# Row maxima of an adjacency matrix: two full passes, or one pass over segments and a gathered window

## The chip, the core and the metric

The kernel runs on one core of a Trainium2 chip. The metric is device time in microseconds (us) of one execution, lower is better. A profile is one execution taken by the hardware profiler; its engines are PE (TensorE's matrix products; PEld its weight loads), DVE (VectorE), ACT (ScalarE), POOL (GpSimd, which here issues the gathers) and SP (which issues most other transfers).

## The reference

Four graph layers on 2708 nodes of 512 features, with one adjacency matrix `adj` (2708x2708, f32, sparse, with a positive diagonal). Cut to what is computed:

```python
# layer 0
h = maximum(layernorm(x), 0)
head = (adj > 0) / max(sqrt(count of adj > 0 in the row), 1e-12)
x = x + ((adj + head) @ h) / rowsum(adj + head)
# layer 1: attention, 8 heads of 64
h = maximum(layernorm(x), 0)
a = maximum(adj, eye)
atts = softmax(q @ k.T / 8 - 1e16 * (1 - a))
x = x + sum over heads (atts @ v) @ Wo
# layer 2
h = maximum(layernorm(x), 0)
h = relu(adj @ (h @ W1) + b1); h = relu(adj @ (h @ W3) + b3)
x = x + tanh(h @ Wf + bf)
# layer 3
h = maximum(layernorm(x), 0)
A = (adj != 0)
x = x + (A @ (h @ W + b)) / colsum(A)
```

The mask of layer 1 multiplies `1 - a` by 1e16, so each row's softmax puts all its weight on the row's largest entry of `max(adj, eye)`. The kernel therefore needs, for each row, the place of that maximum, and the two largest values to see that the maximum stands clear (where it does not, a general version of the whole computation runs, behind a condition at the end; it does not run on these inputs). Layer 1 then is a gather: row i of the result is row `idx[i]` of a table `y = h @ Wv @ Wo`.

## The kernel before, in words

The 2708 rows are 22 row tiles of 128 (the last has 20). Layer 0 goes through the row tiles `m` in a loop (L854). Columns of `adj` that hold many non-zeros are multiplied as whole tiles (`WHOLE[m]` of them); of the rest only the source rows with a non-zero are taken: the kernel counts and ranks them, searches their numbers (`search`, L448, FIND_INDEX8 over a row of ranks), and gathers per row tile `CHUNKS[m]` (5 to 10) pieces of `adj` transposed (`gather_adj`, L635, tile `ac`, 128 runs of 512 bytes) and as many of `h` (`gather_rows`, L654, tile `h`, 16 buffers). Both are indirect DMAs issued by POOL, which works through its list in order. TensorE multiplies the pieces at L866 into `acc`.

Everything that needs a whole row tile of `adj` as rows runs ahead of this loop. `stats_to(k)` (L762) works through the tiles in `order_n` up to tile k: it loads the tile as a slab `ar` (128x2708 f32, three buffers, `load_slab`, L563), takes signs, counts and sums on ScalarE (`row_norm`, `row_sum`), counts columns on TensorE for each group of three (`count`, L325, copied by ScalarE at L341 to L345) and ranks them (`rank_blocks`, L399 to L405, with a small product on TensorE at L403), and then calls `attended`:

```python
nc.vector.tensor_max(ar[:n, cols], ar[:n, cols], ident[:n, :n])
nc.vector.max(tops[:n, m, :], ar[:n])
nc.vector.max_index(at_top[:n, m, :], tops[:n, m, :], ar[:n])
```

L622 is the maximum with the identity on the diagonal block. L623 is one VectorE instruction (MAX8) that gives the eight largest values of 2708; L624 is two, a load of the eight values (MATCH_VALUE_LOAD) and a search for their places (FIND_INDEX8), again over 2708. Six tiles (`LATE`: 3, 4, 5, 0, 1, 2) do not call `attended` in `stats_to`; their slabs are loaded a second time in the last eight turns of the loop (L890 to L895, with `count_signs` on ScalarE).

Behind the loop the places become `idx` (L914), which layer 1's gather of `y` uses (`fetch`, L1172, on POOL); `flags` (L278) compares the two largest values. `after` computes `y` two tiles behind (L176, copied at L810), with a transpose at L210. `norm` (L194 to L204) normalizes the finished rows, first scaled and added at L879. `incidence` builds TensorE's operands on VectorE (L698, L706).

A framework orders the instructions: it records them as the Python program issues them, with their dependencies, and sorts each engine's list by priority and by its own estimate of when each can start. The order on each engine is fixed when the kernel is built. Waits between engines, and between an instruction and the result of another of its own engine, are semaphores that the framework sets. `with tc.issue_after(ins):` adds an edge: what the block issues on `ins`'s engine stands behind `ins` in that engine's list. Tiles of a pool with `bufs=k` take turns in k buffers; a tile that takes a buffer waits until all that used the one before are done.

Of the kernel before, what the change touches and what calls it, by code (L numbers as in the profile page):

```python
# [9 lines left out]
FP = mybir.dt.float32  # L10
# [3 lines left out]
U32 = mybir.dt.uint32  # L14
U8 = mybir.dt.uint8
I32 = mybir.dt.int32
AF = mybir.ActivationFunctionType
ALU = mybir.AluOpType
AX = mybir.AxisListType
# [3 lines left out]
P = 128  # L23
LN_EPS = 1e-5
NORM_EPS = 1e-12
MASK_SCALE = 1e16
# [18 lines left out]
def kernel(  # L45
# [27 lines left out]
    nc = tc.nc  # L73

    N, D = x.shape
    H, _, DK = wk_d.shape
    NT = (N + P - 1) // P
    NFULL = N // P
# [4 lines left out]
    UNIT = 4  # L83
# [81 lines left out]
    nc.gpsimd.memset(ones_b, 1.0)  # L165


    adj_units = bass.AP(adj_t.tensor, 0, [[UNIT, N * N // UNIT], [1, UNIT]])

    def span(t):  # L170
# [73 lines left out]
    with tc.tile_pool(name="l0_slab", bufs=2) as slabs, tc.tile_pool(  # L244
# [15 lines left out]

        idx_a = hp.tile([P, NT, NCH], U32, name="idx_a")

        tops = hp.tile([P, NT, 8], FP, name="tops")
        at_top = hp.tile([P, NT, 8], U32, name="at_top")
        cnts, sums_sgn, ends, caps = (
            hp.tile([P, NT], FP, name=name) for name in ("cnts", "sums_sgn", "ends", "caps")
        )
# [5 lines left out]
        if TAIL:  # L273
            nc.gpsimd.memset(tops[:, NFULL, :], 0.0)
            nc.gpsimd.memset(tops[:, NFULL, 0:1], 2.0)
            nc.gpsimd.memset(at_top[:, NFULL, :], 0)

        def flags():  # L278

            score = wp.tile([P, NT, 2], FP, name="score", bufs=1)  # L280
            nc.vector.tensor_scalar(
                score, tops[:, :, 0:2], 1.0, MASK_SCALE, op0=ALU.subtract, op1=ALU.mult
            )
            nc.vector.tensor_tensor(bad[:, :NT], score[:, :, 1], score[:, :, 0], ALU.is_ge)
            nc.vector.tensor_tensor(
                bad[:, BAD_NEG : BAD_NEG + NT], sums_sgn, cnts, ALU.not_equal
            )
            nc.vector.tensor_tensor(bad[:, BAD_MANY : BAD_MANY + NT], ends, caps, ALU.is_gt)
# [17 lines left out]
        nc.gpsimd.iota(place_i, pattern=[[P, NCH]], base=1, channel_multiplier=1)  # L306
        places = hp.tile([P, NCH], FP, name="places")
        nc.vector.tensor_copy(places, place_i)

        pending, pending_c = [], []  # L310

# [253 lines left out]
        def count_signs(m, last):  # L565

            sgn = slabs.tile([P, N], BF, name="sgn", bufs=GROUP)
            behind(sgn[:1, :1], last)
            nc.scalar.activation(sgn, slab[m], AF.Sign, accum_out=sums_sgn[:, m : m + 1])
            nc.scalar.activation(sgn, sgn, AF.Relu, accum_out=cnts[:, m : m + 1])  # L570
# [46 lines left out]
        def attended(m):  # L617

            n = rows(m)
            cols = slice(m * P, m * P + n)  # L620
            ar = slab.pop(m)
            nc.vector.tensor_max(ar[:n, cols], ar[:n, cols], ident[:n, :n])  # L622
            nc.vector.max(tops[:n, m, :], ar[:n])  # L623
            nc.vector.max_index(at_top[:n, m, :], tops[:n, m, :], ar[:n])  # L624

        gathers, gather_slot = {}, [0]

# [134 lines left out]
        def stats_to(m):  # L762


            while normed[0] <= order_n.index(m):
                t = order_n[normed[0]]
                do_next()
                load_slab(t)
                if normed[0] + 1 < NT:
                    load_slab(order_n[normed[0] + 1])  # L770
                row_norm(t)
                row_sum(t)
                if t == 0 or t % GROUP == GROUP - 1 or t >= NT - 2:
                    last_block = count(masks)
                    if t not in ZERO:
                        if dense_of(t):
                            rank_blocks(list(masks), last_block)
                        else:
                            flush_counts()
                            todo.append(partial(rank_rows, list(masks)))  # L780
                        todo.extend(partial(search, k) for k in masks)
                        do_next(0)
                    masks.clear()
                if t in LATE:
                    slab.pop(t)
                else:
                    attended(t)
                normed[0] += 1
# [65 lines left out]
        for m in range(NT):  # L854
            n = rows(m)
            if m + 1 < NT:
                load_x(m + 1)
            if m + 2 < NT and m + 2 >= LEAD and dense_of(m + 2):
                blocks[m + 2] = load_block(m + 2, tiles_d[: min(dense_of(m + 2), PIECE0)])
            flush()  # L860
            if LEAD <= m + 1 < NT:
                incs[m + 1] = incidence(m + 1)
            acc = ps_acc.tile([P, D], FP, name="acc")
            pairs = incs.pop(m)
            for i, (a, g) in enumerate(pairs):
                product = nc.tensor.matmul(  # L866
                    acc[:n], a, g, start=(i == 0), stop=(i == len(pairs) - 1)
                )
                first_of_sum = first_of_sum if i else product.ins
            if m + 1 < LEAD:  # L870
                stats_to(m + 1)
                incs[m + 1] = incidence(m + 1)
            if m > 1:
                with tc.issue_after(first_of_sum):
                    after(m - 2, None)
            if m:
                after(m - 1, hns.pop(m - 1))
            xt = xs.pop(m)
            nc.vector.scalar_tensor_tensor(  # L879
                xt[:n], acc[:n], row.pop(m)[1][:n], xt[:n], op0=ALU.mult, op1=ALU.add  # L880
            )
            hns[m] = wp.tile([P, D], FP, name="hn")
            norm(wp, xt, n, hns[m])
            store(m, xt)
            if normed[0] == NT:
                do_next(2 if NT - 8 < m < NT - 5 else 1)
            stats_to(min(2 * m + 6, m + 8, NT - 1))
            gathers_to(m + 2)

            step = m - (NT - 8)  # L890
            if 0 <= step < len(LATE):
                load_slab(LATE[step])
            if 0 < step <= len(LATE):
                count_signs(LATE[step - 1], xt[:1, :1])
                attended(LATE[step - 1])  # L895
            if m + 8 == NT + 1:
                todo.append(partial(rank_rows, list(range(1, LEAD))))
                todo.extend(partial(search, k) for k in range(1, LEAD))
            if m == NT // 2:
                load_scores(xt[:1, :1])  # L900
            if m == NT // 2 + 2:
                score_bound(xt[:1, :1])
            if m == NT - LEAD - 1:
                for t in range(1, LEAD):
                    gather_adj(t)
            if m == NT // 2 + 3:
                wr = load_w(wset, w1_d, "wr", lambda w: behind(w[:1, 0, :1], xt[:1, :1]))
            if m == NT // 2 + 5:
                w1 = split_w(
                    wset, wr, "wa", lambda w: behind(w[:1, :1], xt[:1, :1])  # L910
                )
                wr = load_w(wset, w3_d, "wr")
        flush()
        nc.vector.tensor_copy(idx, at_top[:, :, 0])  # L914
        degrees()
        after(NT - 2, None)
        after(NT - 1, hns.pop(NT - 1))
# [1035 lines left out]
```

## Time and profile before

| what | value |
|---|---|
| runs | 1424.02, 1426.85, 1431.88 us; median 1426.85 |
| the profiled execution: its own time, and its span from first to last instruction | 1431.05 us, 1429.2 us |
| mean granted TensorE clock (1 is full speed) | 0.925 |
| PE busy, share of the span | 1218.8 us, 85% |
| DVE | 924.7 us, 65% |
| ACT | 693.2 us, 49% |
| POOL | 673.6 us, 47% |
| layer 0 (0 to 515 us): DVE busy from 100 to 515 | 325.2 us |
| POOL busy from 100 to 515 | 241.7 us |
| L622, L623, L624: first and last start | 99.0 and 498.1 us |

The span is that of the instructions; the own time has a little more around it. Busy time counts no register, branch, semaphore and DMA-issuing instructions of the sequencers. Matmuls are pipelined and their ends are modelled, so a busy PE is not a PE at its peak. In lines of groups the columns are: line, engine, operation, output<-inputs, shape, count | busy us, mean ns of one | idle time of the engine before them and what ended most of it. In a timeline they are start, duration, engine, line, operation, output<-inputs, shape, count and, in brackets, the idle time in front and what ended it.

### The profile page before, as it was taken

What the parts mean: (1) busy time and instruction counts of PE and PEld (TensorE: products, weight loads), DVE (VectorE), ACT (ScalarE), POOL (GpSimd) and SP (SyncE); (2) the same over time, 40 slices, a digit from 0 to 9 for tenths busy, and PEclk for the clock granted to TensorE, in tenths of its full rate; (3) what the DMA queues carried; (4) which work ended last, traced back from release to release, by engine and by line L of the source; (5) the groups of instructions that cost most, each with busy time, mean ns of one, the idle gap of its engine ahead of it and who ended that gap; (6) DMA issues with size and microseconds to landing.
All of it is one profiled execution on the core that took longest, in us unless ns stands there. A gap on an engine that the chain in (4) does not pass through costs nothing. (4 is left out here: it accounts for less than half of the span.)

```text
span 1429.2 us, 15148 instructions
## 1 busy us (share of the span) xinstructions
PE 1218.8 (85%) x4223; PEld 726.3 (51%) x4223; DVE 924.7 (65%) x1859; ACT 693.2 (49%) x1098; POOL 673.6 (47%) x703
## 2 busy tenths in 40 slices
PE   4985977769896848999989999899999999958797
PEld 2332433324343326765655655466666666646575
DVE  4664977768899857952343446356667685746576
ACT  5873563648635636642232224245555554634353
POOL 2245457555667441116645543245445344167663
PEclk9977998789988969999999999999999999979898
DMA  9976898778979477638888887856566666488785
GB/s 342 350 251 225 283 302 277 246 249 293 322 253 335 168 254 266 220 128 272 259 261 255 274 248 239 273 177 219 194 212 193 198 190 207 137 313 249 248 250 163
DMA packets 179342, 349.92 MB, mean 245 GB/s; under 512 B 22795, under 2 KB 85525, under 8 KB 175517
## 3 DMA queue, kind: packets, MB, share of 16 engines
q1 hardware_dynamic: 131648, 201.72, 41.5%
q0 software_dynamic: 46032, 145.05, 32.6%
q10 hardware_dynamic: 1568, 2.10, 0.4%
q8 instruction: 35, 0.57, 0.2%
q14 instruction: 59, 0.48, 0.1%
HBM read 285.97 MB, written 62.82 MB: 244 GB/s over the span
## 5 line engine op out<-in xcount | busy, mean ns | idle before, releaser
L1047 POOL DMA_INDIRECT gg<-g2d,idx_g x130 | 141.2, 1086 | 197.1 <-PE aggs L1110 149.3
L1110 PE MATMUL aggs<-gg,ac 128*128 128x512 f32 (+1 forms) x520 | 231.3, 593 | 3.2 <-DMA gg<-g1d,idx_g 2.1
L1047 POOL DMA_INDIRECT gg<-g1d,idx_g x130 | 130.7, 1005 | 159.1 <-PE aggs L1110 86.5
L635 POOL DMA_INDIRECT ac<-in_adj_t_dram,idx_a x130 | 132.7, 1021 | 91.9 <-issue 37.3
L866 PE MATMUL acc<-h,inc 128*128 128x512 f32 (+1 forms) x276 | 143.0, 664 | 37.4 <-DVE inc L706 29.2
L1110 PEld LDWEIGHTS aggs<-gg,ac 128*128 128x128 f32 (+1 forms) x520 | 97.0, 188 | 113.6 <-issue 102.2
L654 POOL DMA_INDIRECT h<-h0d,idx_g x111 | 114.8, 1034 | 83.7 <-PE acc L866 40.8
L866 PE MATMUL acc<-h,incl 128*128 128x512 f32 (+1 forms) x222 | 106.0, 620 | 0.8 <-issue 0.8
L866 PEld LDWEIGHTS acc<-h,inc 128*128 128x128 f32 (+1 forms) x276 | 54.9, 212 | 101.0 <-issue 60.2
L1075 DVE SCALAR_TENSOR_TENSOR ac<-ac,diag_c,bias 128x512 f32<-128x512 f32 x30 | 22.6, 754 | 100.8 <-DMA ac<-g1d 59.1
L1047 POOL DMA_INDIRECT gg<-hidr,idx_g x62 | 70.7, 1140 | 34.6 <-issue 20.8
L176 PE MATMUL yacc<-wvo,hT 128*128 128x512 f32 (+1 forms) x176 | 83.9, 615 | 1.7 <-ACT hT L211 1.0
L1106 PE MATMUL agg<-ghi,a_hi 128*128 128x512 f32 x180 | 77.3, 429 | 0.0
L1106 PE MATMUL agg<-glo,a_lo 128*128 128x512 f32 x180 | 73.4, 408 | 4.2 <-ACT glo L225 4.2
L1106 PE MATMUL aggs<-gs,a_s 128*128 128x512 f32 x180 | 73.1, 406 | 1.3 <-DVE gs L222 1.3
L990 DVE SCALAR_TENSOR_TENSOR v_lo<-pt,v_hi 128x512 fp32r<-128x512 f32 (+1 forms) x88 | 57.0, 658 | 16.2 <-ACT v_hi L989 13.9
L866 PEld LDWEIGHTS acc<-h,incl 128*128 128x128 f32 (+1 forms) x222 | 41.8, 195 | 50.0 <-issue 47.1
L623 DVE MAX8 tops<-ar 128x8 f32<-128x2708 f32 (+1 forms) x22 | 65.4, 2971 | 0.0
L624 DVE FIND_INDEX8 at_top<-tops,ar 128x8 uint32<-128x2708 f32 (+1 forms) x22 | 65.3, 2969 | 0.0
L989 ACT ACTIVATE v_hi<-pt 128x512 fp32r<-128x512 f32 (+1 forms) x88 | 48.2, 575 | 29.0 <-PE pt L983 22.1
L1139 DVE SCALAR_TENSOR_TENSOR u<-aggs,u 128x512 f32<-128x512 f32 x42 | 28.9, 687 | 50.9 <-PE aggs L1110 37.7
L1010 PE MATMUL main<-wb,v_hi 128*128 128x512 f32 (+1 forms) x176 | 56.7, 444 | 5.2 <-ACT v_hi L989 3.4
(355 smaller groups left out, 2777.9 us busy)
## 6 DMA issues: line engine op xcount, KB each, us to landing
ar<-in_adj_dram SPq DMA_DIRECT2D x27, 1354.0 KB
raw<-in_adj_t_dram SPq DMA_DIRECT2D x92, 192.0 KB
slot<-x SPq DMA_DIRECT2D x41, 256.0 KB
at<-in_adj_t_dram SPq DMA_DIRECT2D x26, 256.0 KB
h<-in_x_dram SPq DMA_DIRECT2D x21, 256.0 KB
h0d<-h POOLq DMA_DIRECT2D x21, 256.0 KB
xt<-in_x_dram SPq DMA_DIRECT2D x21, 256.0 KB
x<-xt SPq DMA_DIRECT2D x21, 256.0 KB
```

What stands on the lines that cost most here:

```text
L176: nc.tensor.matmul(acc[:n], hT[:, c, :n], w[:, c, :], start=(c == 0), stop=(c == NCD - 1))
L623: nc.vector.max(tops[:n, m, :], ar[:n])
L624: nc.vector.max_index(at_top[:n, m, :], tops[:n, m, :], ar[:n])
L635: nc.gpsimd.indirect_dma_start(out=ac[:, c, :n], out_offset=None, in_=adj_units, element_offset=dense_of(m) * P * N + m * P, in_offset=bas ...
L654: nc.gpsimd.indirect_dma_start(out=g, out_offset=None, in_=h0d[:, :], in_offset=bass.IndirectOffsetOnAxis(ap=index_g(m)[:, c : c + 1], axi ...
L866: product = nc.tensor.matmul(acc[:n], a, g, start=(i == 0), stop=(i == len(pairs) - 1))
L989: nc.scalar.activation(hi[d], pt[d], AF.Relu, scale=UP)
L990: nc.vector.scalar_tensor_tensor(lo[d], pt[d], 0.0, hi[d].bitcast(FP), op0=ALU.max, op1=ALU.subtract)
L1010: nc.tensor.matmul(acc[:n], a[:, c, :n], b[:, c, :], start=first and c == 0, stop=last and c == NCD - 1,)
L1047: nc.gpsimd.indirect_dma_start(out=gs[c], out_offset=None, in_=gd[:, :], in_offset=bass.IndirectOffsetOnAxis(ap=index_g(m)[:, c : c + 1], ...
L1106: turn(nc.tensor.matmul(acc[:n], a[:k, i, :n], b[:k], start=st, stop=sp))
L1110: nc.tensor.matmul(mixed[:n], a, g, start=(c == 0 and not dense_of(m)), stop=(c == len(chunks) - 1),)
```

## The change

Full row tiles no longer take the two passes over 2708 elements. `attended` now reduces the row to 22 segment maxima (21 segments of 128 columns in one instruction, the last 20 columns in another), finds the largest segment among the 22, and computes where it begins. One run of 128 elements (512 bytes) a row, from that place on, is gathered from `adj` in HBM by an indirect DMA on POOL. `open_window` then takes the maximum of the gathered run, and its place in the run; the two largest values are the pairwise maximum of the two best segment maxima and the two best in the run. The tile of 20 rows keeps the two passes.

`look` is called once in front of each `attended` (and in turns of the loop without one, and behind the loop until nothing is left). It opens the oldest window when three are under way, or when no segment waits for its gather, and issues the gather of the last segmented tile. Opening a window is put behind `last_segs`, the segment pass of the tile before the present one; with three windows under way that is the pass of the tile three further on than the window's. `tops` and `at_top` become smaller.

```diff
+    row_units = bass.AP(adj.tensor, 0, [[UNIT, N * N // UNIT], [1, UNIT]])
...
-        tops = hp.tile([P, NT, 8], FP, name="tops")
-        at_top = hp.tile([P, NT, 8], U32, name="at_top")
+        tops = hp.tile([P, NT, 2], FP, name="tops")
+        at_top = hp.tile([P, NT], U32, name="at_top")
...
-            nc.vector.max(tops[:n, m, :], ar[:n])
-            nc.vector.max_index(at_top[:n, m, :], tops[:n, m, :], ar[:n])
+            if n < P:
+                high = wp.tile([P, 8], FP, name="high", bufs=1)
+                nc.vector.max(high[:n], ar[:n])
+                where = wp.tile([P, 8], U32, name="where", bufs=1)
+                nc.vector.max_index(where[:n], high[:n], ar[:n])
+                nc.vector.tensor_copy(tops[:n, m, :], high[:n, 0:2])
+                nc.vector.tensor_copy(at_top[:n, m : m + 1], where[:n, 0:1])
+                return
+            segs = wp.tile([P, NT], FP, name="segs", bufs=1)
+            near_w = NFULL * P
+            last_segs[0] = nc.vector.tensor_reduce(
+                segs[:, :NFULL],
+                ar[:, :near_w].rearrange("p (s w) -> p s w", w=P),
+                AX.X,
+                ALU.max,
+            ).ins
+            nc.vector.tensor_reduce(segs[:, NFULL:], ar[:, near_w:], AX.X, ALU.max)
+            peaks = wp.tile([P, 8], FP, name="peaks", bufs=5)
+            nc.vector.max(peaks, segs)
+            best = wp.tile([P, 8], U32, name="best", bufs=1)
+            nc.vector.max_index(best, peaks, segs)
+            begin = wp.tile([P, 1], FP, name="begin", bufs=5)
+            nc.vector.tensor_scalar(
+                begin, best[:, 0:1], float(P // UNIT), float((N - P) // UNIT), op0=ALU.mult, op1=ALU.min
+            )
+            place = wp.tile([P, 1], U32, name="place", bufs=2)
+            nc.vector.tensor_scalar(place, begin, row_unit[:, 0:1], None, op0=ALU.add)
+            segments.append((m, begin, place, peaks))
+
+        segments, windows, last_segs = [], [], [None]
+
+        def open_window(m, begin, win, peaks):
+
+            own = wp.tile([P, 1], FP, name="own_seg")
+            nc.vector.tensor_scalar(
+                own, begin, float(m * P // UNIT), None, op0=ALU.is_equal
+            )
+            nc.vector.scalar_tensor_tensor(
+                win, ident, own[:, 0:1], win, op0=ALU.mult, op1=ALU.max
+            )
+            high = wp.tile([P, 8], FP, name="high", bufs=1)
+            nc.vector.max(high, win)
+            where = wp.tile([P, 8], U32, name="where", bufs=1)
+            nc.vector.max_index(where, high, win)
+            nc.vector.tensor_max(tops[:, m, :], peaks[:, 0:2], high[:, 0:2])
+            nc.vector.scalar_tensor_tensor(
+                at_top[:, m : m + 1],
+                begin,
+                float(UNIT),
+                where[:, 0:1],
+                op0=ALU.mult,
+                op1=ALU.add,
+            )
+
+        def look():
+
+            if windows and (len(windows) == 3 or not segments):
+                with tc.issue_after(last_segs[0]):
+                    open_window(*windows.pop(0))
+            if segments:
+                m, begin, place, peaks = segments.pop(0)
+                win = wp.tile([P, P], FP, name="win", bufs=3)
+                nc.gpsimd.indirect_dma_start(
+                    out=win,
+                    out_offset=None,
+                    in_=row_units,
+                    element_offset=m * P * N,
+                    in_offset=bass.IndirectOffsetOnAxis(ap=place[:, 0:1], axis=0),
+                )
+                windows.append((m, begin, win, peaks))
...
                     masks.clear()
+                look()
                 if t in LATE:
                     slab.pop(t)
                 else:
                     attended(t)
...
             if 0 < step <= len(LATE):
                 count_signs(LATE[step - 1], xt[:1, :1])
+                look()
                 attended(LATE[step - 1])
+            elif normed[0] == NT:
+                look()
...
         flush()
-        nc.vector.tensor_copy(idx, at_top[:, :, 0])
+        while segments or windows:
+            look()
+        nc.vector.tensor_copy(idx, at_top)
```

More of the change, by code (lines that the diff above doesn't have):

```diff
@@ L275 @@
             nc.gpsimd.memset(tops[:, NFULL, 0:1], 2.0)
-            nc.gpsimd.memset(at_top[:, NFULL, :], 0)
+            nc.gpsimd.memset(at_top[:, NFULL:], 0)
         def flags():
@@ L281, in flags @@
             nc.vector.tensor_scalar(
-                score, tops[:, :, 0:2], 1.0, MASK_SCALE, op0=ALU.subtract, op1=ALU.mult
+                score, tops, 1.0, MASK_SCALE, op0=ALU.subtract, op1=ALU.mult
             )
@@ L308 @@
         nc.vector.tensor_copy(places, place_i)
+        row_i = hp.tile([P, 1], I32, name="row_i")
+        nc.gpsimd.iota(row_i, pattern=[[0, 1]], base=0, channel_multiplier=N // UNIT)
+        row_unit = hp.tile([P, 1], FP, name="row_unit")
+        nc.vector.tensor_copy(row_unit, row_i)
         pending, pending_c = [], []
```

## The prediction

> **What bounds the kernel now.** I read the page first, for the span and for where the pass that changes stands among the groups; then the busy times by stretches; then TensorE's waits; then VectorE's timeline around the one long wait of TensorE that VectorE causes.
>
> ```profile
> span 1429.2 us, 15148 instructions
> ...
> L623 DVE MAX8 tops<-ar 128x8 f32<-128x2708 f32 (+1 forms) x22 | 65.4, 2971 | 0.0
> L624 DVE FIND_INDEX8 at_top<-tops,ar 128x8 uint32<-128x2708 f32 (+1 forms) x22 | 65.3, 2969 | 0.0
> ```
>
> The two passes over a whole row tile of adj take 2.97 us each and 130.7 us of VectorE in all. They run from 99.3 us (first L623) to 501.0 us (last L624), in layer 0 only. Everything behind 515 us has none of the changed operations, so I change nothing there: 914 us of the span stay as they are.
>
> In the answer by stretches each engine has busy us and, in brackets, instructions: PE, PEld, DVE, ACT, POOL; then granted clock, DMA share, GB/s.
>
> ```profile
> 145.00:205.00 60.00, 57.17 (x173) 25.89 (x172) 55.66 (x104) 36.94 (x45) 29.09 (x30) 0.97 0.84 276
> ...
> 245.00:260.00 15.00, 0.00 (x0) 0.00 (x0) 0.71 (x3) 1.45 (x4) 8.49 (x9) 0.59 0.35 93
> 259.00:305.00 46.00, 42.94 (x110) 19.60 (x110) 41.91 (x78) 33.23 (x47) 27.22 (x29) 0.94 0.91 307
> 305.00:320.00 15.00, 3.47 (x33) 1.64 (x33) 4.04 (x11) 2.29 (x8) 9.27 (x10) 0.75 0.53 165
> 320.00:383.00 63.00, 62.24 (x187) 28.56 (x188) 58.32 (x112) 46.54 (x65) 38.75 (x40) 0.95 0.92 315
> 395.00:437.00 42.00, 41.15 (x102) 19.02 (x102) 40.05 (x68) 19.40 (x29) 26.58 (x20) 0.93 0.81 275
> 436.00:448.00 12.00, 0.72 (x6) 0.49 (x4) 12.00 (x14) 6.44 (x13) 10.48 (x6) 0.62 0.68 217
> 447.00:490.00 43.00, 41.19 (x102) 18.17 (x103) 40.73 (x70) 23.70 (x28) 21.55 (x21) 0.94 0.74 279
> ```
>
> Two kinds of stretch are to be seen. In the dense ones TensorE is busy 93 to 99% and VectorE 91 to 95%: two nearly equal limits, TensorE slightly the harder. Between them lie holes in which TensorE does next to nothing and its clock falls to 0.59 to 0.75. In two holes (245 to 260, 305 to 320) VectorE is idle as well, and only POOL issues gathers. In the hole from 436 to 448 VectorE is busy without a break.
>
> ```profile
> PE list L403 <- DVE rk L399: 28.4, 3, 15.2
> PE acc L866 <- DVE inc L706: 27.0, 2, 15.7
> PE pt L210 <- ACT hn L204: 7.1, 2, 5.9
> ```
>
> These are TensorE's longest waits between 95 and 515 us (us, times, longest). All name VectorE or ScalarE, but the waits for L399 are not VectorE's making: it waited 30.9 us itself there for ScalarE's copy of the counts (L343). Of the 27.0 us for L706, 15.7 (at 105 to 120 us) lie where VectorE waits 12.9 us too, for a releaser the profile cannot name. What remains to VectorE is the other 11.3 us:
>
> ```profile
> 433.08 4.18 DVE L424 TENSOR_TENSOR_SCAN ar<-ar 3x1940 f16<-3x1940 f16 x1
> 437.19 2.94 DVE L623 MAX8 tops<-ar 128x8 f32<-128x2708 f32 x1
> ...
> 440.78 2.96 DVE L624 FIND_INDEX8 at_top<-tops,ar 128x8 uint32<-128x2708 f32 x1
> ...
> 447.27 0.54 DVE L706 TENSOR_TENSOR inc<-inc,at 128x384 f32<-128x384 f32 x1
> ```
>
> TensorE starts at 447.87, once L706 is through. VectorE is backed up there: 91 to 95% busy since 395, with two pairs L623/L624 from 418 to 444.
>
> **The change, part by part.** The tile of 20 rows keeps its two passes; 21 full tiles change.
>
> *Removed, per tile:* L623 and L624. Start to start (99.26 to 102.16; 160.27 to 163.24 with the value load) they take 2.90 and 2.97: 5.87 us.
>
> *The pass over segments.* No row has a reduction of this size; the only TENSOR_REDUCE (L1514, 67 elements) takes 0.22. From below I take L423, the fastest long pass, 0.85 us for 2708 elements; from above L424's scan, 5.78 for 2708. I take the row nearest in operand and length, L623: one f32 operand read once, 2.90 x 2688/2708 = 2.88 us. The Trainium skill ("VectorE: DVE Perf Modes", Rules for kernel authors) speaks against the change: a reduction runs at one element per cycle and counts as the slowest operation, and one is to keep the number of operations low. At its 0.96 GHz the pass is 2.80 us plus a fixed part, the same as my row; by the second rule the eleven added operations decide, so they are counted one by one.
>
> *The small operations.* After the segment pass come a reduction of 20, MAX8, value load and FIND_INDEX8 over 22, and two scalar operations; at the window one scalar operation, a 128x128 multiply-max, MAX8, value load and FIND_INDEX8 over 128, and two one-column operations. Rows: one-column operations start 0.06 to 0.07 us after each other where none waits; a value load takes 0.07; 128x128 operations 0.20 (L595: 132.69 to 132.90). FIND_INDEX8 takes 2.17 for 1941 and 2.97 for 2709 elements, so 1.04 ns an element, and by that line about 0.28 for 128, or 0.20 start to start. With nothing waiting, an estimate from these: behind the pass 3 x 0.08 (20 and 22 elements) + 0.07 + 2 x 0.07 = 0.45, at the window 3 x 0.20 + 0.07 + 3 x 0.07 = 0.88; 1.33 us together. Where each of eight needs the result in front, it starts after that one's end, some 0.1 later (L622 to L623: 0.29 apart, where 0.20 is usual): 2.1 us. The tile then costs 2.88 + 1.33 = 4.2 to 5.0 instead of 5.87. The trace shows VectorE's list well mixed (other tiles' operations stand between L623 and L624), so I take the middle: **1.2 us saved per tile, 25 us of VectorE in 21 tiles**, with 17 and 35 as ends.
>
> *What becomes of it.* In the dense stretches (254 us) TensorE is busy 96%: the saving turns into idle time of VectorE. I give it 2 us of the 9 that TensorE is idle there. In the holes in which VectorE itself waits (105 to 120, 245 to 260, 305 to 320) it buys nothing. At 436 two to three late tiles lie in the backlog: 3 us of the 11.3. At the end, the wait of 5.9 for L204 stands behind tile 1's L624 (487.11 to 490.00) and tile 2's L623, which delay L879 and the shift: about 2 us. Sum: **7 us**.
>
> *Moved and added elsewhere.* 21 gathers on POOL. L635's rows say 0.94 us each, 1.25 start to start: 26 us of POOL, 58% busy between 100 and 515 us, so mostly into its idle time (it waits 40.8 us for TensorE at L654). Behind each stand the L635 and L654 gathers of the next row tiles. In three stretches POOL issues back to back towards a hole (188 to 208, 232 to 255, 298 to 316); one window more there is 1.25 us later for all behind it: I charge 2 of 3.75 us. SP gains: a slab comes free one pass earlier (its waits for L624: 9.2 us), but ScalarE waits for a slab's load only 1.2 us, so I price that at nothing. On VectorE the window's operations wait for a gather issued three row tiles before, some 45 us at 14.5 us a tile (L210 starts at 267.84, 282.35 and 297.33); the one landing the chain shows is 4.71 us, so that wait costs nothing. Queued behind it, should it not hold, would be the next tile's L698 and L706, and behind them TensorE.
>
> *The end.* The last window is issued after the last pass, at about 499 us, among POOL's L635 gathers (494 to 505), and three windows are opened after it. idx is needed at 514.58 (L1172). Last pass at 499, issue by 505, 4.7 to land, 1.3 for the window: 511. 3.5 us in hand, cost nothing; without them the end slips by what is missing.
>
> Net 7 - 2 = 5 us, against the profiled execution's own time: 1431.05 (span 1429.2) becomes 1426. That execution lies at the top of the three runs, whose median is 1426.85; the same 5 us from there give **1422 us**. What a measurement can tell from no change is about 0.5%, 7 us: the forecast lies inside it, near its edge.
>
> **Rivals.**
> 1. *VectorE is the real limit of the dense stretches.* Matmul ends are modelled, so 96% may hide waits. For it: 91 to 95% of VectorE, no gap in it from 395 to 437. Then most of the 25 us come back, also in the dense stretches: 15 to 25 us, 1402 to 1412, say 1408. Against it: TensorE's small waits there for VectorE are 0.7 to 1.7 us each.
> 2. *POOL is held up (slower).* POOL executes in order, and the window's gather needs its place from VectorE and a free window buffer, both behind a segment pass. Where VectorE is later than the order assumed, POOL stands still, with L635 and L654 of the next tile behind it. A tile has 12 to 14 gathers, 15 to 17.5 us at 1.25, against TensorE's 14.5: POOL has no room in a dense stretch. Price 1.25 us for the gather plus part of a pass of 2.9: 2 to 3 us on 8 tiles or so, 16 to 24 us against the gain of 7: +9 to +17, 1436 to 1444, say 1438. It decides where POOL's wait in front of the window exceeds what its 16 buffers of h ahead of TensorE cover.
> 3. *It doesn't do what it says:* the small operations wait for each other and the windows are opened bunched; 1425 to 1430.
>
> **How the numbers follow.** Forecast (1414 to 1426) 0.42, rival 1 0.22, rival 2 0.26, rival 3 0.10. The holes with no named releaser, 10 to 16 us each, can move with any change of order; that widens every case. The range reaches into both outer cases: 1403 to 1442. Faster by over 0.5% is below 1419.7: 0.18 of the forecast's 0.42, and rival 1: 0.40. Slower is above 1434: rival 2, 0.26. The rest, 0.34, is within 0.5%.
>
> **What would show it.** The pass over segments at 2.8 to 3.0 us and VectorE's busy time down by some 25 us (and not 17 or 35); the wait of TensorE near 436 shorter by 3; dense stretches as long as before. Rival 1: the dense stretches shorter. Rival 2: POOL's window gathers waiting for the place operation, and TensorE's waits naming gathers. I am wrong if the reduction takes far from 2.9 us, or if a hole comes or goes.

## The result and the profile after

The changed kernel takes 1439.30 us (median of 17 runs, 1429.28 to 1446.62). The kernel before, on the same chips, takes 1428.48 (17 runs, 1422.27 to 1440.12). The ratio is 1.0062, 95% interval 1.0033 to 1.0092: **slower by 0.6%, about 9 us** (the medians lie 10.8 us apart). The forecast was 5 us faster. The profiled execution took 1441.61 us, its span is 1439.7.

The page of the changed kernel, span, busy times and pass over segments:

```profile
span 1439.7 us, 15424 instructions
...
PE 1217.5 (85%) x4223; PEld 726.2 (50%) x4223; DVE 897.8 (62%) x2093; ACT 693.3 (48%) x1098; POOL 697.1 (48%) x725
...
L639 DVE TENSOR_REDUCE segs<-ar 128x21 f32<-128x2688 f32 x21 | 61.8, 2942 | 3.0 <-remote 2.5
```

The pass takes 2.94 us where 2.88 were worked out. VectorE's busy time fell from 924.7 to 897.8 us, 26.9 less where 25 were forecast. So VectorE did get its time back. The two kernels in the same stretch of layer 0, first before, then after (us of the stretch; busy us of PE, PEld, DVE, ACT, POOL with instructions in brackets; granted clock, DMA share, GB/s):

```profile
95.00:515.00 420.00, 330.47 (x968) 148.38 (x966) 330.17 (x607) 226.83 (x316) 245.51 (x242) 0.88 0.78 263
```

```profile
95.00:515.00 420.00, 327.33 (x912) 147.35 (x910) 289.38 (x773) 215.15 (x299) 253.51 (x250) 0.87 0.78 258
```

VectorE is busy 41 us less in these 420 us, 27 by the change, the rest because less got done: TensorE ran 912 instructions instead of 968. Nothing that VectorE gave up shows as more work of TensorE, which is busy 3 us less. TensorE's waits from 95 to 525 us in the changed kernel (us, times, longest), to be read beside those of before:

```profile
PE list L409 <- DVE rk L405: 23.3, 3, 15.9
PE list L605 <- DVE deg L618: 17.8, 1, 17.8
PE rb L550 <- issue: 9.5, 1, 9.5
PE acc L941 <- DVE inc L780: 8.8, 4, 4.0
```

The wait for `inc` fell from 27.0 to 8.8, but L605 (a one-column product for a row tile's diagonal) and L550 (a product of `score_bound`) have long waits that they did not have. The hole at 436 to 448 (11.3 us) is now three, at 452, 462 and 467, of 4.7, 3.9 and 4.0. The first product of layer 1 starts at 550.4 us instead of 528.7.

How far single profiles carry: behind that product the lists of TensorE and VectorE are those of before, but for operations early in layer 1 (compared for several kernels), and there the profiled executions of this study last 888 to 902 us. Differences of under some 10 us between single profiles of the whole are not read. The verdicts below are the ratios on record, each between runs of both kernels on the same chip or chips. They are not the quotients of the medians, which lie some 0.3% off at most: 1.0076 for the changed kernel, 1.0049 for gather_only, 1.0064 for sp_twice. Runs that took over 1.5% more than the fastest of their kernel are left out of the ratios, among them four of pool_time's twelve with the profiled one; the quotient of its medians, all twelve counted, is 0.9982.

### The profile page after: what moved, and what is told of

It reads as the page before. It is cut to its first block, busy times and chain, and to the rows that moved or that the text cites. A ratio compares the mean times of both kernels' runs of the same rounds, so it can differ in the third digit from the quotient of the medians.

```text
span 1439.7 us, 15424 instructions
## 1 busy us (share of the span) xinstructions
PE 1217.5 (85%) x4223; PEld 726.2 (50%) x4223; DVE 897.8 (62%) x2093; ACT 693.3 (48%) x1098; POOL 697.1 (48%) x725
## 5 line engine op out<-in xcount | busy, mean ns | idle before, releaser
L728 POOL DMA_INDIRECT h<-h0d,idx_g x111 | 111.4, 1004 | 85.9 <-PE acc L941 35.7
L941 PE MATMUL acc<-h,incl 128*128 128x512 f32 (+1 forms) x222 | 101.1, 603 | 0.0
L1127 POOL DMA_INDIRECT gg<-hidr,idx_g x62 | 74.4, 1199 | 33.1 <-issue 17.4
L639 DVE TENSOR_REDUCE segs<-ar 128x21 f32<-128x2688 f32 x21 | 61.8, 2942 | 3.0 <-remote 2.5
L177 PEld LDWEIGHTS yacc<-wvo,hT 128*128 128x128 f32 (+1 forms) x176 | 33.9, 197 | 50.8 <-issue 46.4
```

What stands on the lines that cost most here:

```text
L177: nc.tensor.matmul(acc[:n], hT[:, c, :n], w[:, c, :], start=(c == 0), stop=(c == NCD - 1))
L639: last_segs[0] = nc.vector.tensor_reduce(segs[:, :NFULL], ar[:, :near_w].rearrange("p (s w) -> p s w", w=P), AX.X, ALU.max,).ins
L728: nc.gpsimd.indirect_dma_start(out=g, out_offset=None, in_=h0d[:, :], in_offset=bass.IndirectOffsetOnAxis(ap=index_g(m)[:, c : c + 1], axi ...
L941: product = nc.tensor.matmul(acc[:n], a, g, start=(i == 0), stop=(i == len(pairs) - 1))
L1127: nc.gpsimd.indirect_dma_start(out=gs[c], out_offset=None, in_=gd[:, :], in_offset=bass.IndirectOffsetOnAxis(ap=index_g(m)[:, c : c + 1], ...
```

## The experiments

"Layer 1" is the start of layer 1's first product in the profile of that run; the kernel before, on the chips used, had medians of 1428.5 to 1438.5 us. 1% is 14.3 us.

| run | median us | ratio to before, 95% interval | layer 1 at, us |
|---|---|---|---|
| (kernel before, first and second profile) | | | 528.7, 531.4 |
| (changed kernel) | 1439.30 | 1.0062 (1.0033 to 1.0092) | 550.4 |
| win_first | 1449.07 | 1.0110 (1.0078 to 1.0142) | 550.7 |
| last_two | 1445.41 | 1.0082 (1.0057 to 1.0108) | 551.9 |
| late_two | 1441.13 | 1.0038 (1.0013 to 1.0063) | 544.2 |
| late_seg | 1424.16 | 0.9941 (0.9913 to 0.9969) | 530.6 |
| late_seg_again | 1420.00 | 0.9879 (0.9850 to 0.9909) | 527.1 |
| no_drain | 1436.91 | 1.0013 (0.9982 to 1.0044) | 547.0 |
| mid_no_drain | 1441.23 | 1.0027 (1.0000 to 1.0054) | 546.0 |
| no_window | 1425.56 | 0.9933 (0.9907 to 0.9960) | 535.5 |
| one_pass | 1424.48 | 0.9920 (0.9883 to 0.9957) | 538.5 |
| gather_only | 1443.05 | 1.0082 (1.0043 to 1.0122) | 545.8 |
| gather_twice | 1453.82 | 1.0180 (1.0123 to 1.0237) | 564.7 |
| gather_small | 1439.41 | 1.0042 (1.0006 to 1.0078) | 542.7 |
| gather_mid | 1441.34 | 1.0038 (1.0003 to 1.0073) | 544.5 |
| gather_late | 1431.05 | 0.9969 (0.9939 to 0.9999) | 534.3 |
| pool_time | 1427.15 | 0.9954 (0.9916 to 0.9992) | 535.0 |
| sp_twice | 1445.45 | 1.0035 (1.0003 to 1.0067) | 551.1 |

### First theory: the end of layer 0

The trace after shows something plain at the end. VectorE's timeline:

```profile
529.97 0.35 DVE L666 SCALAR_TENSOR_TENSOR win<-ident,own_seg,win 128x128 f32<-128x128 f32 x1 [12.62 <-DMA win<-in_adj_dram,place]
...
532.80 0.18 DVE L994 COPY idx<-at_top 128x22 uint32<-128x22 uint32 x1
```

VectorE stands 12.62 us in front of the last windows, whose gathers POOL issued at 527.20 and 528.50, behind nine gathers and two stores of row tile 2. `idx` is ready at 532.8, the first fetch of layer 1 at 536.9. The wait looks like 7 to 8 us of loss. win_first puts tile 2's gathers behind the windows:

```diff
-                for t in range(1, LEAD):
+                for t in range(1, LEAD - 1):
                     gather_adj(t)
...
         while segments or windows:
             look()
+        with tc.issue_after(last_win[0]):
+            gather_adj(LEAD - 1)
```

> The changed kernel with one thing altered: on POOL the nine last gathers of pieces of adj (row tile 2) and their two stores stand behind the two last window gathers instead of in front of them; the lists of the other engines in layer 0 are the same. B is the time of the kernel before on this chip; the changed kernel stands at about B + 9. Theory 1 (the loss is made at the end of layer 0, where the last windows stand at the end of POOL's list): the last window lands at about 521 instead of 529.9, idx is ready by 524 instead of 532.8, the first fetch of layer 1 is then held by POOL's own list (11 issues, some 15 us behind the windows) at about 532 instead of 536.9: 5 us faster than the changed kernel, B + 4. Theory 2 (the loss is made in the middle, by window gathers that hold POOL up, 230 to 510 us): within 2 us of the changed kernel, B + 9. Theory 3 (the holes in which all engines but POOL stand still move with any change of order): no forecast of the sign, but here the order in front of 515 us is the same, so the holes must be the same too.

The window waits are gone, and `idx` is ready at 520.7, twelve us earlier. The first fetch is at 536.2, where it was. VectorE's timeline in win_first shows why:

```profile
520.74 0.18 DVE L996 COPY idx<-at_top 128x22 uint32<-128x22 uint32 x1
...
531.03 0.18 DVE L374 TENSOR_TENSOR rdeg<-list,has 128x21 f32<-128x21 f32 x1 [10.01 <-remote]
```

L374 waits for column sums by TensorE, whose last matmul ends at 525.6 in the profile; TensorE's semaphore update for it is recorded at 531.01. Behind L374 stand a bias load and, on the same SP queue, the last store of `y` (532.6), and the fetch needs that store; behind L374 stand also the operations on `wb` (L218 to L226, the last of VectorE's over at 536.16) whose ends the fetch waits for as well. So the end had a second wait, just behind the first, and the theory falls: taking the first one away gave nothing. last_two and late_two test the same end by keeping two passes in the last two or in all six late tiles:

```diff
-            if n < P:
+            if n < P or m in (1, 2):   # last_two; late_two: m in LATE; late_seg: m not in LATE
```

> The changed kernel, but the two row tiles attended last (1 and 2) keep the two passes of the kernel before; 19 tiles use segments. Theory 1: no window gather stands at the end of POOL's list, idx follows the last pass as before, the first fetch comes some 4 us behind the last product of y instead of 11.7: 7 us saved, 2 us given back by two longer tiles on VectorE, so 5 us faster than the changed kernel: B + 4. Theory 2: 2 of 21 window gathers are gone, so about 1 us of the 9: B + 8. Theory 3: holes as in the changed kernel up to about 470 us.

Not faster either (1.0082). The six late tiles without segments, and the complement:

> The changed kernel, but all six late tiles (3, 4, 5, 0, 1, 2) keep the two passes; the other 15 full tiles use segments. Theory 1: the end is as in the kernel before, and only what the 15 tiles save or cost in the middle is left: B to B + 2. Theory 2: 15 of 21 window gathers stay and with them 15/21 of the loss: B + 6. Theory 3: anywhere within B - 10 to B + 10, with TensorE's long waits in front of 330 us as in the changed kernel.

> The complement: only the six late tiles use segments and windows; the other 15 full tiles keep two passes. Theory 1: the whole loss at the end is here, 7 us, less some 3 us that the late tiles save VectorE near 436: B + 5 to B + 8. Theory 2: 6 of 21 window gathers, so 6/21 of the loss: B + 2 to B + 3. Theory 3: holes in front of 330 us as in the kernel before.

**late_seg is faster than both kernels**, by 0.6% (0.3 to 0.9), which none of the three theories had, though it has the same end with the last windows behind a wait of 8.1 us. late_two, without any window at the end, stays slow, by 0.4% (0.1 to 0.6). What late_two shows of the loss is made by the 15 tiles that go through `stats_to`, in front of 415 us, and theory 1 is wrong by place. The two halves do not add up to the whole (0.4 less 0.6%, against 0.6% slower): the parts are not worth the same apart as together.

### Which part of it, in the middle

In four profiles (after, win_first, last_two, late_two) VectorE also stands still once in the middle. The timeline of the changed kernel:

```profile
384.38 0.37 DVE L666 SCALAR_TENSOR_TENSOR win<-ident,own_seg,win 128x128 f32<-128x128 f32 x1
...
395.48 0.35 DVE L666 SCALAR_TENSOR_TENSOR win<-ident,own_seg,win 128x128 f32<-128x128 f32 x1 [10.55 <-issue]
```

That window's gather was issued at 389.43: when no further tile has a segment ready, `look` opens the windows at once, not three tiles later. no_drain opens them only when three are out:

```diff
-            if windows and (len(windows) == 3 or not segments):
+            if len(windows) == 3 or (windows and closing[0]):
```

> The changed kernel, but a window is opened only when three are out (or behind the loop), and no longer at once when no further row tile has a segment ready; the lists are the same up to about 382 us. In four profiles (the changed kernel, win_first, last_two, late_two) VectorE stands 10.5 to 10.8 us at 385 to 395 us in front of one window whose gather was issued only 6 us earlier, and TensorE has a hole of 7 to 9.5 us behind it (401 to 411). Theory W (that wait is a main part of the loss): the wait and the hole go, the end of layer 0 comes 6 to 9 us earlier than in the changed kernel, and the time is 5 to 9 us under the changed kernel's, B to B + 4, where B is the kernel before and the changed kernel stands at B + 9. Theory P (the gathers on POOL in the loop cost it, whatever waits for them): B + 8 to B + 10, as the changed kernel. Theory S (VectorE's shorter passes only move the holes): the hole comes back elsewhere, B + 9.

It came out at 1.0013, which fits theory W, against the changed kernel's 1.0062, though the intervals overlap (0.9982 to 1.0044, and 1.0033 to 1.0092). Three runs with it take the change apart. gather_only adds only the 21 gathers to the kernel before:

```diff
             nc.vector.max_index(at_top[:n, m, :], tops[:n, m, :], ar[:n])
+            if n == P:
+                place = wp.tile([P, 1], U32, name="place", bufs=2)
+                nc.vector.tensor_scalar(
+                    place, tops[:, m, 0:1], 0.0, row_unit[:, 0:1], op0=ALU.mult, op1=ALU.add
+                )
+                segments.append((m, place))
```

(`look` then issues the gather as in the change and opens no window.)

> The kernel before with both its passes, and 21 gathers of windows added on POOL at the places of the changed kernel, each behind one operation of one column on VectorE behind the tile's passes; nothing reads the windows, and no segments are taken. Theory W: POOL's gathers alone cost little, B to B + 3 (21 x 1.25 us in POOL's idle time, 21 x 0.07 us on VectorE). Theory P: the gathers carry the loss: B + 7 to B + 12, and the stretches in which all engines but POOL stand still are longer than in the kernel before.

**The gathers alone cost 0.82% (0.43 to 1.22)**, with VectorE's work as before: theory P. (What the new order of the lists has in this comes under the next heading.) no_window keeps the segments and drops gathers and windows:

```diff
-            segments.append((m, begin, place, peaks))
+            nc.vector.tensor_copy(tops[:, m, :], peaks[:, 0:2])
+            nc.vector.tensor_copy(at_top[:, m : m + 1], begin)
```

> The changed kernel without windows: the pass over segments, the maximum over 22 and its place stay, the gathers on POOL and the operations on the gathered segment are left out, and the place written is the start of the segment, not the place in it. VectorE saves some 2.4 us a tile, 50 us in all. Theory W: no wait for a window is left, so the loss goes: at or under the kernel before, B - 10 to B. Theory P: the same, B - 10 to B, as the gathers are gone too. Theory S (less work on VectorE in the loop is worth nothing there, and the new order or the chain of waits on VectorE's own results costs): B + 3 to B + 9.

one_pass prices VectorE's time by itself:

```diff
-            nc.vector.max_index(at_top[:n, m, :], tops[:n, m, :], ar[:n])
+            if n < P:
+                nc.vector.max_index(at_top[:n, m, :], tops[:n, m, :], ar[:n])
+            else:
+                nc.vector.tensor_copy(at_top[:, m, 0:1], places[:, 0:1])
```

> The kernel before, but the 21 full tiles keep only the first of their two passes; in place of the search for the place stands a copy of one column (the places are left out). VectorE saves 2.9 us a tile, 61 us in all, and nothing is added on any engine. It measures what VectorE's time in the loop is worth by itself. Theory W and theory P: VectorE's time is worth something, most of it behind 415 us: B - 12 to B - 5. Theory S: B - 2 to B + 9.

VectorE's busy time falls by 45.0 us in no_window and 56.7 in one_pass, and the time by 0.67 and 0.80%, 9.6 and 11.5 us: 0.2 us of time for 1 us of VectorE. Theory S is out. By that price the change's 26.9 us are worth about 5. The price is not cleared of order: in both kernels the lists of layer 0 stand in another order than before, and in their profiles layer 1 starts later than in the kernel before, not sooner.

Was it the wait after all that no_drain took away? mid_no_drain takes it away in late_two, where the late tiles stay as they are; the last windows are put behind late tiles' passes:

```diff
-                nc.vector.max(high[:n], ar[:n])
+                last_segs[0] = nc.vector.max(high[:n], ar[:n]).ins
```

> late_two (segments in the 15 tiles in front of the late ones, two passes in the six late tiles; it stood 5.4 us over the kernel before, B) with the windows opened only when three are out, the last ones behind the passes of late tiles. Theory W (the wait of 10.5 us in front of one window costs 5 to 9 us): the wait at 385 to 395 us goes, B - 3 to B + 1. If the wait was covered after all and no_drain was faster by its other order: B + 4 to B + 6.

The wait is gone (no L666 between 381.5 and 399.9 us, and the one at 399.92 did not wait), and TensorE's hole is there all the same. mid_no_drain's waits of TensorE from 390 to 420 us:

```profile
PE rb L550 <- issue: 7.0, 1, 7.0
```

Its ratio is 1.0027 beside 1.0038 for late_two: no difference that can be told, and with 0 to 8 us over the kernel before the ratio alone does not decide between the two expectations. The trace speaks against theory W: without the wait TensorE stands there as long, and layer 1 starts no sooner (546.0, for 544.2), so VectorE's 10.5 us were covered. The hole at L550 is 4 to 10 us long in all eight kernels in which the 15 tiles' passes are shorter (no_window 8.2 and one_pass 6.6 among them), and 0 to 3.3 in the kernel before and late_seg. But holes of 7.1 to 10.4 us stand there too, at the next `rb` product behind L550, in gather_mid, pool_time and sp_twice, which keep both passes; the hole is no mark of the shorter passes. Where it stands at L550, TensorE's list holds L550 in front of other products, and its input comes from ScalarE's L548, which runs late there. Why no_drain stands lower than the changed kernel stays open; the two were not run on one chip.

### What of a gather costs

First a second profile of the kernel before:

> The kernel before once more, for a second profile. Layer 0 ends (first product of layer 1) at 528.7 us in the first profile, but at 535.5 and 538.5 in the profiles of no_window and one_pass, which are faster over all. If the first profile was a short one of layer 0, this one shows 535 to 545 us there and a shorter rest; if not, 527 to 531 us.

Layer 1 starts at 531.4, so 528.7 was no exception. The kernel before has a short layer 0 in both its profiles, shorter than in four kernels that are faster by their ratios (no_window, one_pass, gather_late, pool_time); I can't explain that, and read the last column of the table only for large differences.

pool_time replaces each gather by POOL time without a transfer:

```diff
-                nc.gpsimd.indirect_dma_start(
...
+                for _ in range(5):
+                    nc.gpsimd.memset(place, 0.0)
```

> As gather_only, but in place of each of the 21 gathers stand five small fills of a tile on POOL (128x200 each, about 1.3 us together), which wait for the same operation of VectorE and move no data by DMA. B is the kernel before, gather_only stood at B + 11. Theory T (what a gather costs is POOL's time in its list): B + 8 to B + 13, as gather_only. Theory D (what a gather costs is its transfer: descriptors, bytes, or what they do to the arrival of semaphore updates): B to B + 3.

> As gather_only, but each window is gathered twice: 42 gathers. Theory T and theory D, if the cost is by the gather: B + 20 to B + 25. If only a few places decide (a single train of gathers that becomes too long): B + 10 to B + 15.

gather_small takes `out=win[:, :UNIT]`:

> As gather_only, but each of the 21 gathers takes 16 bytes a row instead of 512: the same number of issues and of descriptors, 1/32 of the bytes. Theory T, and theory D in so far as it is issues and descriptors: B + 8 to B + 12. Theory D in so far as it is bytes: B to B + 3.

The rows of gather_only and of pool_time (line, engine, operation, count | busy us, mean ns | idle before):

```profile
L644 POOL DMA_INDIRECT win<-in_adj_dram,place x21 | 20.9, 997 | 9.8 <-issue 5.2 <-DVE place L633 4.0 <-DVE rdeg L377 0.3
```

```profile
L644 POOL MEMSET place<- 128x200 f32 x105 | 28.5, 272 | 11.8 <-DVE place L633 8.2
```

The fills keep POOL busy longer than the gathers (28.5 against 20.9 us) and make it wait longer for the place (8.2 against 4.0), and pool_time is not slower than the kernel before (0.9954). **POOL's time is not the price** (theory T is out). The price goes with the gathers: 0 at none, 0.8% at 21, 1.8% at 42. With 1/32 of the bytes it is 0.4%, with an interval (0.1 to 0.8) that reaches from almost nothing to the whole.

Is it the order of the lists rather than the gathers? The traces answer this. Apart from what was added, the lists of VectorE, ScalarE and POOL in gather_only, gather_small, gather_twice and pool_time are the same, instruction for instruction. (In the kernel before, 100 of VectorE's 1859 and 66 of ScalarE's 1098 instructions stand elsewhere; TensorE's records differ among the four in 2 to 11 of 4223 places, and in 5 between the two profiles of the kernel before.) So these four differ by the gathers, and the order is no rival among them. From pool_time to gather_only it is an estimated 1.3%, to gather_twice 2.3%, by the ratios; 0.7 and 1.9% by the quotients of the medians. The same instruction of VectorE, near the end of layer 0, in pool_time, gather_only and gather_twice:

```profile
513.09 0.18 DVE L374 TENSOR_TENSOR rdeg<-list,has 128x21 f32<-128x21 f32 x1 [6.41 <-PE list L365]
```

```profile
524.11 0.18 DVE L374 TENSOR_TENSOR rdeg<-list,has 128x21 f32<-128x21 f32 x1 [5.95 <-PE list L365]
```

```profile
542.31 0.18 DVE L374 TENSOR_TENSOR rdeg<-list,has 128x21 f32<-128x21 f32 x1 [6.53 <-PE list L365]
```

It comes 11.0 and 29.2 us later. At L405 the distance to pool_time's 133.90 us is 3.4 and 10.7, at its 181.16 us 5.5 and 17.5, at 252.34 us 8.0 and 24.0, and at 307.28 us 11.1 and 26.3; up to 393 us it swings (6 to 19, 24 to 38), and from there on it stays at 11 to 12 and 29 to 31. So the delay is made in front of about 390 us, most of it by 310, which gather_mid and gather_late put to the test below; these are single profiles.

The next runs ask for bytes and for place. sp_twice moves gather_twice's bytes by plain loads on SP's queue:

```diff
+                for _ in range(2):
+                    win = wp.tile([P, P], FP, name="win", bufs=3)
+                    nc.sync.dma_start(out=win, in_=adj[m * P : m * P + P, m * P : m * P + P])
```

> The kernel before with 42 loads added on SP's queue, each a block of 128 rows of 512 bytes of adj, as much as the 42 gathers of gather_twice carry (which stood at B + 24), spread over layer 0, read by nothing. Theory X (the transfers of layer 0 are near their limit, the DMA share is 0.81 to 0.92 in the dense stretches of the kernel before, and any added transfer lengthens it): B + 15 to B + 25. Theory G (what costs is that the transfer is a gather issued by POOL): B to B + 5.

gather_mid and gather_late change one condition of gather_only (`n == P and m not in LATE`, `n == P and m in LATE`):

> As gather_only, but only the 15 tiles in front of the late ones have a gather. If each gather costs the same, 15/21 of 11.7 us: B + 8. If the cost is made in the dense stretches in front of 415 us, all of it: B + 12.

> As gather_only, but only the six late tiles have a gather. If each gather costs the same, 6/21 of 11.7 us: B + 3. If the cost is made in front of 415 us: B.

The same 2.75 MB cost 0.35% (0.03 to 0.67) on SP's queue, where the order is that of the kernel before, and 1.8% (1.2 to 2.4) as gathers: mostly theory G, with a part for the transfer. (By the medians it is 0.64% and 1.68%. In its one profile sp_twice starts layer 1 some 20 us later than the kernel before; the times of its runs do not show a loss of that size.) The 15 gathers in the middle cost 0.4% (0.0 to 0.7) over the kernel before, and an estimated 0.8% over pool_time, whose order gather_mid has but for one instruction each of VectorE and ScalarE; the six late ones nothing (0.3% faster, in the order of before). That gathers are free there fits late_seg's gain, but does not explain it: its VectorE is busy 918.7 us for 924.7, and 6.0 us are worth 1 us at the price above, not 8. late_seg once more:

> late_seg once more, on another chip: the version with segments in the six late tiles alone, B - 8.4 in its first measurement. If its gain is real: B - 12 to B - 4. If it was the scatter between chips: B - 3 to B + 3.

1.2% faster (0.9 to 1.5) on this chip. The gain is real, and here larger than was expected; its size lies between 0.3 and 1.5%. What makes it stays open: the lists of layer 0 stand in another order there too, and in the two profiles layer 1 starts no sooner (530.6 and 527.1) than in the kernel before (528.7 and 531.4).

## Why the prediction was wrong, step by step

- *The pass over segments and the small operations*: right. 2.94 us for 2.88; 26.9 us of VectorE for 25. (5.87 less 5.0 in 21 tiles makes the lower end 18, not 17, and the row tile has 2708 elements, not 2709.)
- *What becomes of it*: 7 us of 25 was about right, as far as no_window and one_pass show it: 0.2 us per us, 5 us for 26.9, not cleared of order. Rival 1 (15 to 25 us) is out: 45.0 and 56.7 us less on VectorE gave 9.6 and 11.5. The place of the gain was wrong in part: the hole at 436 did not shrink by 3 us but split into 12.6 us of holes. In late_seg it does shrink, from 11.3 to 9.3. And the prediction's own sign of being wrong, "if a hole comes or goes", was there: 17.8 us at L605.
- *Moved and added elsewhere*: **this is the step that failed.** "26 us of POOL, 58% busy between 100 and 515 us, so mostly into its idle time", charged at 2 us. Measured alone, the 21 gathers cost 0.82%, 11.7 us (6 to 17), the new order of the lists included, and more beside pool_time, which has that order. I priced a gather by the time that POOL spends issuing it. pool_time shows that this time is free, as the step said; the gather is not.
- *"So that wait costs nothing"* (the window's gather, issued some 45 us ahead): wrong as a fact and right as a sum. One wait of 10.55 us came where the windows are drained early, which I had read in `look` ("or when no segment waits") and not followed to the tile where it happens. In mid_no_drain it is gone and TensorE stands as long, so it was covered.
- *The end*: "3.5 us in hand", 511 us. It was 532.8, because the whole layer came later and POOL's list had nine gathers and two stores in front of the last windows. win_first shows that this wait, too, was no loss by itself: another wait, for TensorE, ended as late.
- *Rival 2* has the sign and the size (1438 for 1439.3), with the wrong mechanism: POOL held up by place and buffer. POOL waited 10.3 us in front of window gathers for VectorE's operations on segments and windows (`tops` 5.3, `peaks` 3.9, `segs` 1.1), but pool_time has 8.2 us of such waits and is not slower than before. Size and sign were luck.
- The parts add up within their intervals, no closer: VectorE's relief without windows -9.6 us, gathers +11.7, and the window operations on VectorE, which give back some of the relief (no_window saves 45.0 us, the change 26.9: 18 us at 0.2, +4), make +6 where +9 were measured. No run takes the gathers alone out of the changed kernel with its order kept; for that kernel itself the cause is this sum.

What stays open: how a gather in the middle lengthens layer 0. The difference between gathers and plain loads is shown, the way is not. pool_time and gather_late add work, and both are 0.3 to 0.5% faster than the kernel before, pool_time in another order, gather_late in the same. Effects of that size can't be told here from a lucky order or from scatter.

## What the runs showed of the hardware that I had not expected

**Results arrive late in some stretches.** In the hole of 17.8 us at L605, VectorE works off its list, and neither TensorE nor ScalarE computes. The timeline of the changed kernel (start, duration, and in brackets the idle time in front):

```profile
233.01 0.09 DVE L649 MATCH_VALUE_LOAD best<-peaks,segs 128x8 f32 x1 [2.84 <-remote]
233.09 0.17 DVE L649 FIND_INDEX8 best<-peaks,segs 128x8 uint32<-128x22 f32 x1
233.18 0.67 DVE L780 TENSOR_TENSOR inc<-inc,at 128x512 f32<-128x512 f32 x1
...
235.84 0.15 DVE L651 TENSOR_SCALAR begin<-best 128x1 f32<-128x1 uint32 x1 [1.99 <-issue]
235.91 1.08 DVE L780 TENSOR_TENSOR incl<-incl,ac 128x896 f32<-128x896 f32 x1
...
238.64 0.21 DVE L655 TENSOR_SCALAR place<-begin,row_unit 128x1 uint32<-128x1 f32 x1 [1.65 <-remote]
...
245.66 0.19 PE L605 MATMUL list<-ones_b,sgn 128*128 128x1 bf16 x1 [17.80 <-DVE deg L618]
```

L649 needs only VectorE's own `peaks` (MAX8 from 228.81 to 228.99), and starts 4.0 us after it ended. L651 needs L649's place and starts 2.6 us after it; L655 needs `begin` and starts 2.65 us after. At 215 to 217 us three links of the same chain each start within 0.6 us of the end of the one in front. In the holes an engine's own result reaches it microseconds late, and TensorE's update of 531.01 above is the same kind. The kernel before has such holes as well (its waits for L403). During them POOL issues gathers without a pause. That is coincidence in time and no cause shown: the stretches of layer 0 in which an update is recorded over 0.8 us after the last instruction that could have made it (overlapping ones counted once) come to 53 and 59 us in the two profiles of the kernel before, 52 in pool_time, 93 after, 91 in gather_only, but only 64 in gather_twice, which is the slowest.

The Trainium skill ("VectorE: DVE Perf Modes", Rules for kernel authors) says of chained operations to minimize their count and not their semaphores. At 215 to 217 us, where results come at once, this case agrees: a link costs 0.6 us at most. In this hole it does not: a link that waits costs 2.6 to 4.0 us, while an operation that waits for nothing (L780 at 233.18 and 235.91) costs its own time, so there the number of links in a row counts, eight per tile in this change.

## What to carry to other kernels

Price an added gather by a run of its own, not by the time in which its engine issues it: POOL was free for 28.5 us of fills and not for 21 gathers of 64 KB. Build the control so that the lists keep their order, as gather_only and pool_time do beside each other: one added operation a tile moved 100 of VectorE's 1859 instructions here. An engine that is 95% busy beside another that is 96% busy returned little of what was saved on it, here about a fifth, and a small price elsewhere ate that. And a long wait in a trace is a loss only when it is shown to be: two waits of over 10 us were taken away here, and the next wait stood right behind each.
